# Layer 3's preparation spread over its steps, and a bank of TensorE filled between two halves of a sum

## The chip, the cores and the metric

The kernel runs on one core of one Trainium2 chip. The metric is device time in microseconds (us), the median of several runs. One further execution was recorded by the hardware profiler; all profile lines come from it.

## The reference

A small network of four layers runs on a batch of four images, each 256 channels of 64 x 64 points. Every layer normalizes its input in groups of channels, computes something, and adds it to its input. Layers 0 to 2 (a deformable convolution, an attention, a second deformable aggregation) are not touched. Layer 3 is a selective state space model over the 4096 points of an image in sequence, here cut to what matters:

```python
xz = einsum('bld,ed->ble', xs, in_proj_w)             # 256 -> 2 * 512
u, res = split(xz, 2)
u = silu(causal_depthwise_conv(u, conv_w) + conv_b)   # 4 taps
dt, Bm, Cm = split(einsum('bld,ed->ble', u, x_proj_w), [16, 32])
delta = softplus(einsum('blr,dr->bld', dt, dt_proj_w) + dt_proj_b)
# for each of 512 channels d and 16 states n, along the sequence l:
state = exp(delta * A[d, n]) * state + delta * Bm[n] * u
y = sum_n(state * Cm[n]) + u * D
out = einsum('ble,de->bld', y * silu(res), out_proj_w)
```

## The kernel before

The images are worked one after the other, and within an image the layers. `layer3` cuts the sequence into NC = 8 chunks of C = 512 points. The 512 channels lie as four quarters `dc` of 128 partitions. A chunk is worked in 16 steps, one for each state n, so an image has 128 steps `s`. In one step:

- TensorE (PE) spreads row n of B over the partitions: `bn`, one matmul in bf16 (`state`, L1460). `bn` has a single PSUM bank.
- VectorE (DVE) multiplies `h = du * bn` (the product, L1537), for all four quarters (128x2048) or for three (128x1536). In the second case GpSimd (POOL) multiplies the fourth (`quarter`, L1468) with a row `bs` that a DMA has spread. The list `helped` says in which steps: 14, 15 and 0 to 5 of each chunk.
- ScalarE (ACT) computes `da = exp(delta * A)` for each quarter (L1547), into one of two PSUM banks, and DVE scans over the points (L1548), four scans a step.
- POOL copies the last column to `carry` (L1560) and multiplies `h` by the spread row of C, `cn` (L1563).
- PE adds `h` into four PSUM banks `y` with an identity matrix as weights (`add`, L1438), two steps later. In state 0 it also adds `u * D` (L1436).

`front(j)` prepares chunk j while chunk j-1 is worked: the normalized input `xn`; four projections into `up`, through the one PSUM bank of the pool `ps` (`project`, matmuls L1242, copies L1246); four convolutions, each as four matmuls with diagonal weights (`convolve`, L1285, copied by ACT at L1290); SiLU of `u` and of the gates of the chunk before, with a load of ACT's tables before and after (`silu`, L1299, L1258; called the table visit below); the product that gives dt, B and C (`shares`, L1309, copied to `dbc`); `step` (L1324, ACT at L1330 and L1331), and then a softplus in whole-tile steps, of which ACT does the functions and POOL three additions (L1346, L1355, L1356) and `du = delta * u` (L1357). `gate` projects the other half of `xz`, and `split` cuts B into bf16 parts. `close(j)` multiplies the finished `y` by the gates and projects them to the output, after `gated` (L1514, four products on DVE).

Each part is put by hand into a slot: a step and a half of it. `front(j)` starts LEAD = 4 steps before chunk j; for chunk 1, prepared in part by `first`, 2 steps are taken off. The main loop fixes the order on every engine, as the pools are under a manual schedule; in short:

```python
product; empty(s, -1); gated
scan(0); scan(1); quarter(s + 1)
empty(s, 0)          # second PE parts of the slot, and ACT's copy of the bank
fill(s, 1)           # PE's part of the second half
scan(2); scan(3)
empty(s, 1)
carry; h * cn; empty(s, 2)
state(s + 1); add(s - 2); fill(s + 1, 0)
```

All engines take their queues in order. `first()` prepares chunk 0 by itself before the steps begin: quarters 1 and 3 are convolved by DVE (L1159, L1161), 0 and 2 by PE (L1177); POOL casts the weights `pick` (L1110) and normalizes `xn` of chunk 1 (L1169); then, quarter by quarter, softplus passes from ACT (L1220 to L1222, L1215) to DVE (L1223, L1224, L1216, L1217) and POOL (L1227, L1209 to L1212).

Of the kernel before, what the change touches and what calls it, by code (L numbers as in the profile page):

```python
# [16 lines left out]
P = 128  # L17
# [46 lines left out]
class Net:  # L64
# [1016 lines left out]
    def layer3(self, x, out, nxt, early):  # L1081
# [5 lines left out]

        nc, tc = self.nc, self.tc
        C = 512
        NC, LEAD = N // C, 4  # L1090
        with (
# [18 lines left out]
            nc.gpsimd.tensor_copy(pick.rearrange("p n m -> p (n m)"), rows.rearrange("p a b -> p (a b)"))  # L1110
# [9 lines left out]
            kept = pa.tile([P, 2, C], F32, tag="kept", name="kept")  # L1120
# [9 lines left out]
            def first():  # L1130
# [23 lines left out]
                for dc in range(4):  # L1154
                    pu = spare()
                    project(pu, xn, dc)
                    if dc % 2:
                        nc.vector.tensor_copy(up[:, dc, 3:], pu)
                        nc.vector.tensor_scalar_mul(u[:, dc, :], up[:, dc, :C], cw[:, dc, 0:1])  # L1159
                        for i in range(1, 4):  # L1160
                            nc.vector.scalar_tensor_tensor(  # L1161
                                u[:, dc, :], up[:, dc, i : i + C], cw[:, dc, i : i + 1], u[:, dc, :], ALU.mult, ALU.add
                            )
                    else:
                        nc.scalar.copy(up[:, dc, 3:], pu)
                for ct in range(2):
                    if ct == 0:
                        c1["xn"] = pa.tile([P, 2, C], F32, tag="xn3", name="xn3")
                    nc.gpsimd.tensor_scalar(  # L1169
                        c1["xn"][:, ct, :], x[:, ct, C : 2 * C], rs[:, ct : ct + 1], shift[:, ct : ct + 1], ALU.mult, ALU.add  # L1170
                    )
                nc.gpsimd.tensor_copy(tail, up[:, :, C : C + 3])
                px = bank()
                for dc in (0, 2):
                    cv = spare()
                    for i in range(4):
                        nc.tensor.matmul(cv, conv[:, dc, i, :], up[:, dc, i : i + C], start=(i == 0), stop=(i == 3))  # L1177
                    nc.scalar.activation(u[:, dc + 1, :], u[:, dc + 1, :], AF.Silu, bias=cb[:, dc + 1 : dc + 2])
                    nc.scalar.activation(u[:, dc, :], cv, AF.Silu, bias=cb[:, dc : dc + 1])
                for k, dc in enumerate((1, 3, 0, 2)):  # L1180
                    nc.tensor.matmul(px, xpw[:, dc, :], u[:, dc, :], start=(k == 0), stop=(k == 3))
# [17 lines left out]

                c["gates"] = [spare() for _ in range(4)]  # L1200
                for dc, pg in enumerate(c["gates"]):
                    project(pg, xn, 4 + dc)
# [5 lines left out]
                def split(lo, hi):  # L1208
                    nc.gpsimd.tensor_copy(bp[lo:hi], dbc[lo:hi])  # L1209
                    if hi < P:  # L1210
                        nc.gpsimd.tensor_copy(t[hi:], dbc[hi:])
                        nc.gpsimd.tensor_sub(dbc[hi:], dbc[hi:], t[hi:])  # L1212

                def end(dc):
                    nc.scalar.activation(w[:, dc, :], w[:, dc, :], AF.Ln)  # L1215
                    nc.vector.tensor_add(delta[:, dc, :], delta[:, dc, :], w[:, dc, :])  # L1216
                    nc.vector.tensor_mul(du[:, dc, :], delta[:, dc, :], u[:, dc, :])  # L1217

                for dc in range(4):
                    nc.scalar.activation(w[:, dc, :], pzs[dc], AF.Abs, bias=dtb[:, dc : dc + 1])  # L1220
                    nc.scalar.activation(du[:, dc, :], w[:, dc, :], AF.Exp, scale=-1.0)
                    nc.scalar.activation(delta[:, dc, :], pzs[dc], AF.Relu, bias=dtb[:, dc : dc + 1])  # L1222
# [4 lines left out]
                    nc.gpsimd.tensor_sub(delta[:, dc, :], delta[:, dc, :], du[:, dc, :])  # L1227
                    if dc < 3:
                        split(*((0, 64), (64, 96), (96, 128))[dc])
                    if dc:  # L1230
                        end(dc - 1)
                end(3)
                for dc in range(3):
                    nc.scalar.copy(c1["up"][:, dc, 3:], pus[dc])

# [24 lines left out]
            def front(j):  # L1260
# [17 lines left out]
                for dc in range(4):  # L1278
                    put((dc + 1) // 2, (dc + 1) % 2, *project(j, dc, lambda dc=dc: c["up"][:, dc, 3:]))

                def convolve(dc):
# [7 lines left out]
                    def rest():  # L1289
                        nc.scalar.activation(c["u"][:, dc, :], c["b"], AF.Identity, bias=cb[:, dc : dc + 1])  # L1290
                        if dc == 0:
# [4 lines left out]
                for dc in range(4):  # L1296
                    put(2 + dc, 1, *convolve(dc))
# [5 lines left out]
                put(6, 0, None, silu)  # L1303
# [14 lines left out]
                put(7, 1, shares, keep)  # L1318
# [16 lines left out]
                for dc in range(4):  # L1335
                    put(8 + dc // 2, dc % 2, *step(dc))
                put(10, 0, None, lambda: nc.scalar.activation(c["du"], c["du"], AF.Exp, scale=-1.0))

                def one():
                    c["w"] = pa.tile([P, 4, C], F32, tag="w3", name="w3")  # L1340
                    nc.scalar.activation(c["w"], c["du"], AF.Identity, bias=self.ones[:, 0:1])

                put(10, 1, None, one)


                put(10, 2, None, lambda: nc.gpsimd.tensor_add(c["delta"], c["delta"], c["du"]))  # L1346
                put(
                    12,
                    0,
                    None,  # L1350
                    lambda: nc.scalar.activation(c["du"], c["w"], AF.Identity, bias=self.ones[:, 0:1], scale=-1.0),
                )
                put(13, 0, None, lambda: nc.scalar.activation(c["w"], c["w"], AF.Ln))
                last = 17 if j > 1 else 15
                put(13, 2, None, lambda: nc.gpsimd.tensor_add(c["delta"], c["delta"], c["du"]))  # L1355
                put((13 + last) // 2, 2, None, lambda: nc.gpsimd.tensor_add(c["delta"], c["delta"], c["w"]))  # L1356
                put(last, 2, None, lambda: nc.gpsimd.tensor_mul(c["du"], c["delta"], c["u"]))  # L1357

                for dc in range(4):
                    at = ((14, 0), (14, 1), (15, 0), (15, 1)) if j > 1 else ((10, 1), (11, 0), (11, 1), (12, 1))  # L1360
                    put(*at[dc], *gate(j, dc))
# [19 lines left out]
                for i in range(3):  # L1381
                    put((11, 12, 14)[i], i % 2, None, split(i))
                return todo

            def close(j):
# [5 lines left out]
                def project(ot):  # L1391
                    def pe():
# [6 lines left out]
                        xs = kept[:, ot, :] if last else x[:, ot, bass.ts(j, C)]  # L1399
                        nc.tensor.matmul(c["b"], self.ident, xs, start=False, stop=True)  # L1400

                    def rest():
                        to = kept if last else x[:, :, bass.ts(j, C)]
# [5 lines left out]
                for ot in range(2):  # L1409
                    todo.append((11 + 2 * ot - LEAD, 1, *project(ot)))  # L1410
                if not last:
                    todo.append((15 - LEAD, -1, None, lambda: fetch(j)))

                    todo.append((13 - LEAD + DS if j < NC - 2 else 17 - LEAD, -1, None, lambda: count(j)))
# [12 lines left out]
            def keep():  # L1427
                for ct in range(2):
                    nc.scalar.copy(kept[:, ct, :], x[:, ct, bass.ts(NC - 1, C)])

            def add(j, n, h):
                c = chunks[j]
                if n == 0:
                    c["ys"] = [py.tile([P, C], F32, tag="y", name="y") for _ in range(4)]
                    for dc in range(4):
                        nc.tensor.matmul(c["ys"][dc], diag[:, dc, :], c["u"][:, dc, :], start=True, stop=False)  # L1436
                for dc in range(4):
                    nc.tensor.matmul(c["ys"][dc], self.ident, h[:, dc, :], start=False, stop=(n == DS - 1))  # L1438


            hs, helped = {}, (14, 15, 0, 1, 2, 3, 4, 5)
# [261 lines left out]
```

## Time and profile before

| | |
|---|---|
| time, median of 3 runs | 9832.72 us (9831.53 to 9837.35) |
| the profiled execution: its time | 9825.3 us |
| its span, first to last instruction | 9823.5 us |
| busy: PE, DVE, ACT, POOL | 8552.6, 7522.1, 4893.9, 7112.0 us |
| mean granted clock of TensorE | 0.959 |
| first product of layer 3, image 1 and image 4 | at 1563.67 and 8864.99 us |
| last instruction of DVE's scans, image 4 | starts at 9792.2 us |

A line of a timeline gives start and length in us, engine, line of the kernel, operation, output and inputs, and how many instructions are merged; in brackets stands the idle time of the engine just before, and what ended it. A line of a group of instructions ends with busy time, mean duration in ns, and idle time before. A line of the windows gives, for a stretch of time, each engine's busy time.

### The profile page before, as it was taken

The page shows a single profiled execution, that of the slowest core. Times are in us where ns is not written, and L with a number is a line of the kernel's source. Part 1 is how long each engine was busy: PE and PEld are TensorE (multiplying, and loading weights), DVE is VectorE, ACT ScalarE, POOL GpSimd, SP SyncE. Part 2 cuts the span into 40 slices and gives each one's busy share as a digit, 9 for nine tenths or more (in the row PEclk, how much of TensorE's full clock was granted, in tenths as well). Part 3 has the DMA queues.
Part 4 walks back from the last instruction along what each step waited for, and adds up shares of the span by engine and source line. Part 5 has one row for each costly group of instructions (what it writes and reads, how often), then busy time and mean ns, then how long its engine had stood idle before and what let it go on. Part 6 is the DMA issues. An engine that isn't in the chain of part 4 may idle for free. (4 is left out here: it accounts for less than half of the span.)

```text
span 9823.5 us, 89566 instructions
## 1 busy us (share of the span) xinstructions
PE 8552.6 (87%) x29129; PEld 4208.7 (43%) x29129; DVE 7522.1 (77%) x8175; ACT 4893.9 (50%) x7532; POOL 7112.0 (72%) x4220
## 2 busy tenths in 40 slices
PE   5789998998778999899878899989987889998997
PEld 3643343333464344333346434433334643443333
DVE  4764498999676459899968645989996764689998
ACT  3753335665474333566547433266655733326664
POOL 3746687888474668798857467789985746778997
PEclk9999999999899999999989999999998999999999
DMA  7840011222783001122279201122228820111221
GB/s 255 319 158 1 26 50 56 64 62 67 257 320 139 1 30 47 58 63 63 67 272 333 107 1 35 51 57 62 62 64 313 324 73 1 39 51 55 60 60 51
DMA packets 415274, 1024.78 MB, mean 104 GB/s; under 512 B 38771, under 2 KB 111916, under 8 KB 412748
## 3 DMA queue, kind: packets, MB, share of 16 engines
q0 software_dynamic: 165888, 604.05, 17.0%
q1 hardware_dynamic: 248908, 414.90, 13.7%
q8 instruction: 233, 3.82, 0.2%
q14 instruction: 245, 2.01, 0.1%
HBM read 851.70 MB, written 93.37 MB: 96 GB/s over the span
## 5 line engine op out<-in xcount | busy, mean ns | idle before, releaser
L1548 DVE TENSOR_TENSOR_SCAN h<-da,carry,h 128x512 f32<-128x512 f32 x2048 | 2469.0, 1264 | 138.3 <-ACT da L1547 78.0
L1563 POOL TENSOR_TENSOR h<-h,cn 128x2048 f32<-128x2048 f32 x508 | 2299.7, 4527 | 41.3 <-POOL carry L1560 0.8
L1547 ACT ACTIVATE da<-delta,l3a 128x512 f32<-128x512 f32 x2048 | 1393.1, 689 | 1064.1 <-DVE h L1548 1061.5
L1438 PE MATMUL y<-h,ident 128*128 128x512 f32 x4096 | 1907.6, 610 | 12.4 <-POOL h L1563 12.4
L344 POOL DMA_INDIRECT g<-tab,idx x1152 | 1359.8, 1180 | 748.6 <-issue 367.5
L565 POOL TENSOR_TENSOR acc<-acc,e 128x1024 f32<-128x1024 f32 x480 | 1126.0, 2346 | 539.5 <-ACT e L561 517.6
L388 PE MATMUL pz<-cols,l0w 128*128 128x256 f32 x4608 | 1211.3, 409 | 184.6 <-DVE cols L377 73.9
L1438 PEld LDWEIGHTS y<-h,ident 128*128 128x128 f32 x4096 | 801.7, 196 | 1251.6 <-issue 1166.7
L353 DVE SCALAR_TENSOR_TENSOR r<-g,wx,r 128x512 f32<-128x512 f32 x1152 | 858.4, 745 | 373.4 <-ACT r L352 251.4
L462 DVE TENSOR_REDUCE m<-pm 128x3 f32<-128x1536 f32 (+2 forms) x340 | 599.5, 1763 | 699.9 <-PE pm L452 699.9
L1537 DVE TENSOR_TENSOR h<-du,bn 128x2048 f32<-128x2048 f32 (+1 forms) x512 | 1022.8, 1998 | 49.9 <-PE bn L1460 49.8
L388 PEld LDWEIGHTS pz<-cols,l0w 128*128 128x128 f32 x4608 | 893.2, 204 | 353.7 <-DVE cols L377 110.4
L561 ACT ACTIVATE e<-sc 128x1024 f32<-128x1024 f32 x512 | 496.1, 1020 | 1029.5 <-PE sc L548 1029.5
L572 PE MATMUL cx<-e,v 128*128 128x512 f32 x2048 | 1001.0, 616 | 0.0
L845 DVE TENSOR_TENSOR prod<-ring,A 128x1280 f32<-128x1280 f32 x640 | 922.4, 1480 | 77.9 <-DMA ring<-ring 60.2
L352 ACT ACTIVATE r<-g,wx 128x512 f32<-128x512 f32 x1152 | 826.5, 717 | 265.0 <-DMA g<-tab,idx 211.6
L862 PE MATMUL pacc<-prod,ident 128*128 128x512 f32 x1920 | 914.5, 611 | 32.8 <-DVE prod L845 21.8
L854 POOL TENSOR_TENSOR prod<-prod 128x512 f32<-128x512 f32 x640 | 801.2, 1277 | 182.2 <-DVE prod L845 157.3
L370 PE MATMUL pt<-ident,acc 128*128 128x128 f32 x2304 | 428.3, 293 | 295.0 <-DVE acc L361 234.2
L572 PEld LDWEIGHTS cx<-e,v 128*128 128x128 f32 x2048 | 352.4, 189 | 599.3 <-issue 596.8
L360 ACT ACTIVATE acc<-r,wy 128x256 f32<-128x256 f32 x1152 | 571.3, 496 | 16.5 <-DVE r L353 13.7
L361 DVE SCALAR_TENSOR_TENSOR acc<-r,wy,acc 128x256 f32<-128x256 f32 x1152 | 548.6, 477 | 0.0
(255 smaller groups left out, 10767.4 us busy)
## 6 DMA issues: line engine op xcount, KB each, us to landing
cn<-cd SPq DMA_DIRECT2D x512, 256.0 KB
tab<-vt SPq DMA_DIRECT2D x112, 640.0 KB
bs<-cd SPq DMA_DIRECT2D x256, 256.0 KB
ring<-ring SPq DMA_DIRECT2D x288, 126.0 KB
ring<-ring SPq DMA_DIRECT2D x288, 124.0 KB
g<-tab,idx POOLq DMA_INDIRECT x1152
x<-in_x SPq DMA_DIRECT2D x64, 256.0 KB
out<-x SPq DMA_DIRECT2D x56, 256.0 KB
```

The lines of the kernel that those rows point to most:

```text
L344: nc.gpsimd.indirect_dma_start(out=g[:], out_offset=None, in_=tab[:, :], in_offset=bass.IndirectOffsetOnAxis(ap=idx[:, t, k : k + 1], axis=0),
L353: nc.vector.scalar_tensor_tensor(r, g[:, :, 1, :], wx[:, 1, t, k : k + 1], r, ALU.mult, ALU.add)
L388: nc.tensor.matmul(sums[m][:, ot, :256], wf[:, i, bass.ts(ot, P)], cols[m][:, i, :], start=(i == 0), stop=(i == 17),)
L565: nc.gpsimd.tensor_add(b["acc"], b["acc"], e)
L572: nc.tensor.matmul(blocks[qb]["cx"], v[:, 4 * (i + kt // 4 * 4) + kt % 4, :], e[:, bass.ts(i % 2, 512)], start=(kt == 0 and i == 0), stop= ...
L845: nc.vector.tensor_mul(d["prod"][:, :, t, :].rearrange("p x (g c) -> p x g c", c=GC), ring[y // VR % 4][:, :, y % VR, :].rearrange("p x (g ...
L862: nc.tensor.matmul(d["pd"], self.ident, prod[:, wx, :], start=(wy == 0 and wx == 4), stop=(wy == WIN - 1 and wx == 2),)
L1438: nc.tensor.matmul(c["ys"][dc], self.ident, h[:, dc, :], start=False, stop=(n == DS - 1))
L1537: nc.vector.tensor_mul(h[:, :d, :], c["du"][:, :d, :], c.pop(("bn", n)).to_broadcast([P, d, C]))
L1547: nc.scalar.activation(da, c["delta"][:, dc, :], AF.Exp, scale=al[:, dc, n : n + 1])
L1548: nc.vector.tensor_tensor_scan(h[:, dc, :], da, h[:, dc, :], carry[:, dc, n : n + 1], ALU.mult, ALU.add)
L1563: nc.gpsimd.tensor_mul(h, h, cn.to_broadcast([P, 4, C]))
```

## The change

All of it is in `layer3`.

- The slots move. LEAD is 5. Projections of `up` stand at steps (counted from the first) 0, 1, 1 and 4 instead of 0 to 2; convolutions at 2, 3, 5 and 6 instead of 2 to 5; SiLU, `shares`, `step` and most of the softplus one step later than in the old count, thus at the same step of the chunk before; for chunk 1 one step later. Some parts of ACT move by half a step. Gates and `close` come one step earlier.
- In the main loop `state(s + 1)` moves from the end of the step to between the scans. `add` is cut into two halves of two quarters, and `fill(s + 1, 0)` goes between them. Where the slot's first half holds nothing for PE, `fill(s, 1)` goes ahead of `state`.
- At the steps of the table visit (`visits`) DVE makes the next step's product between scans 1 and 2. bn_stats of the next image's input (`count`) moves there too for most chunks.
- `quarter` writes a tile of its own, `hq`; steps 14 and 15 of chunk 0 are no longer helped.
- In `first`, DVE convolves quarters 1, 3 and 0, PE only 2. `pick`, `xn` of chunk 1 and the casts of `split` go from POOL to ACT. Relu and Ln write PSUM in place, and DVE makes the subtraction of POOL. The gates' projections follow `state(0)`.
- `kept` uses the buffer of `xn3`.

```diff
-        NC, LEAD = N // C, 4
+        NC, LEAD = N // C, 5
...
-                for dc in range(4):
+                c1["xn"] = pa.tile([P, 2, C], F32, tag="xn3", name="xn3")
+                for dc in (1, 3, 0, 2):
                     pu = spare()
                     project(pu, xn, dc)
-                    if dc % 2:
+                    if dc == 1:
                         nc.vector.tensor_copy(up[:, dc, 3:], pu)
+                    else:
+                        nc.scalar.copy(up[:, dc, 3:], pu)
+                    if dc != 2:
                         nc.vector.tensor_scalar_mul(u[:, dc, :], up[:, dc, :C], cw[:, dc, 0:1])
...
+                    if dc == 3:
+                        nc.scalar.copy(pick.rearrange("p n m -> p (n m)"), rows.rearrange("p a b -> p (a b)"))
...
+                px, cv = bank(), spare()
+                for i in range(4):
+                    nc.tensor.matmul(cv, conv[:, 2, i, :], up[:, 2, i : i + C], start=(i == 0), stop=(i == 3))
+                for k, dc in enumerate((1, 2, 3, 0)):
+                    nc.scalar.activation(u[:, dc, :], cv if dc == 2 else u[:, dc, :], AF.Silu, bias=cb[:, dc : dc + 1])
                     nc.tensor.matmul(px, xpw[:, dc, :], u[:, dc, :], start=(k == 0), stop=(k == 3))
...
                 def end(dc):
-                    nc.scalar.activation(w[:, dc, :], w[:, dc, :], AF.Ln)
-                    nc.vector.tensor_add(delta[:, dc, :], delta[:, dc, :], w[:, dc, :])
+                    nc.scalar.activation(pzs[dc], w[:, dc, :], AF.Ln)
+                    nc.vector.tensor_add(delta[:, dc, :], pzs[dc], delta[:, dc, :])
                     nc.vector.tensor_mul(du[:, dc, :], delta[:, dc, :], u[:, dc, :])
...
-                    nc.gpsimd.tensor_sub(delta[:, dc, :], delta[:, dc, :], du[:, dc, :])
-                    if dc < 3:
-                        split(*((0, 64), (64, 96), (96, 128))[dc])
+                    nc.vector.tensor_sub(delta[:, dc, :], pzs[dc], du[:, dc, :])
                     if dc:
                         end(dc - 1)
+                        split(*((0, 64), (64, 96), (96, 128))[dc - 1])
...
                 for dc in range(4):
-                    put((dc + 1) // 2, (dc + 1) % 2, *project(j, dc, lambda dc=dc: c["up"][:, dc, 3:]))
+                    at = ((0, 1), (1, 0), (1, 1), (4, 1))[dc]
+                    put(*at, *project(j, dc, lambda dc=dc: c["up"][:, dc, 3:]))
...
                 for dc in range(4):
-                    put(2 + dc, 1, *convolve(dc))
+                    at = ((2, 1) if j > 1 else (3, 0), (3, 1), (5, 1), (6, 1))[dc]
+                    put(*at, *convolve(dc))
...
-                put(6, 0, None, silu)
+                put(7, 0, None, silu)
+                visits.append(DS * (j - 1) + (2 if j > 1 else 5))
...
-                last = 17 if j > 1 else 15
-                put(13, 2, None, lambda: nc.gpsimd.tensor_add(c["delta"], c["delta"], c["du"]))
-                put((13 + last) // 2, 2, None, lambda: nc.gpsimd.tensor_add(c["delta"], c["delta"], c["w"]))
-                put(last, 2, None, lambda: nc.gpsimd.tensor_mul(c["du"], c["delta"], c["u"]))
+                last = 18 if j > 1 else 16
+                put(14, 2, None, lambda: nc.gpsimd.tensor_add(c["delta"], c["delta"], c["du"]))
+                put((14 + last) // 2, 2, None, lambda: nc.gpsimd.tensor_add(c["delta"], c["delta"], c["w"]))
+                put(last, 2, None, lambda: nc.gpsimd.tensor_mul(c["du"], c["delta"], c["u"]))
...
-            hs, helped = {}, (14, 15, 0, 1, 2, 3, 4, 5)
+            hs, helped = {}, [s for s in range(NC * DS) if s % DS in (14, 15, 0, 1, 2, 3, 4, 5) and s // 2 != 7]
...
                     scan(0)
                     scan(1)
                     quarter(s + 1)
+
+                    free = not any(pe or rest.__name__ == "begin" for pe, rest in slots.get((s, 0), ()))
+                    if free:
+                        fill(s, 1)
+                    state(s + 1)
+                    if s in visits:
+                        product(s + 1)
                     empty(s, 0)
-                    fill(s, 1)
+                    if not free:
+                        fill(s, 1)
                     scan(2)
                     scan(3)
                     empty(s, 1)
...
-                    state(s + 1)
                     late.append((j, n, h))
-                    if len(late) > 2:
-                        add(*late.pop(0))
+
+                    a = late.pop(0) if len(late) > 2 else None
+                    if a:
+                        add(*a, 0)
                     fill(s + 1, 0)
+                    if a:
+                        add(*a, 1)
```

`product(s)` is the old product, moved into a function that does nothing where it has already been called.

## Prediction before the run

> **What bounds the kernel now.** Only layer 3 changes; it runs once per image, four times. First I read the windows by stage of the last image's layer 3, cut at the first product of each chunk.
>
> ```profile
> core 0: us, PE busy (x) PEld busy (x) DVE busy (x) ACT busy (x) POOL busy (x), PEclk, DMA share, GB/s
> 8818.00:8865.00 47.00, 37.93 (x85) 16.47 (x85) 29.98 (x41) 21.00 (x33) 29.92 (x39) 0.93 0.23 77
> 8865.00:8984.60 119.60, 100.22 (x230) 41.92 (x231) 108.12 (x81) 75.90 (x106) 97.50 (x47) 0.99 0.17 47
> ...
> 9215.80:9332.40 116.60, 107.00 (x253) 45.78 (x253) 110.51 (x85) 74.35 (x103) 105.61 (x49) 1.00 0.20 60
> ```
>
> A middle chunk takes 116.6 us; DVE is busy 110.5 of it, PE 107.0, POOL 105.6. DVE paces it, with little room behind. Its gaps are in the timeline of DVE at the end of one chunk and the start of the next:
>
> ```profile
> 9201.25 1.73 DVE L1537 TENSOR_TENSOR h<-du,bn 128x1536 f32<-128x1536 f32 x1
> 9203.08 4.81 DVE L1548 TENSOR_TENSOR_SCAN h<-da,carry,h 128x512 f32<-128x512 f32 x4
> 9208.74 1.75 DVE L1537 TENSOR_TENSOR h<-du,bn 128x1536 f32<-128x1536 f32 x1 [0.85 <-PE bn L1460]
> ...
> 9215.82 1.75 DVE L1537 TENSOR_TENSOR h<-du,bn 128x1536 f32<-128x1536 f32 x1 [0.42 <-PE bn L1460]
> ...
> 9238.71 2.46 DVE L1548 TENSOR_TENSOR_SCAN h<-da,carry,h 128x512 f32<-128x512 f32 x2 [2.21 <-ACT da L1547]
> 9241.08 1.73 DVE L1537 TENSOR_TENSOR h<-du,bn 128x1536 f32<-128x1536 f32 x1
> ...
> 9247.64 1.73 DVE L1537 TENSOR_TENSOR h<-du,bn 128x1536 f32<-128x1536 f32 x1
> ```
>
> A free step with a 3-wide product lasts 6.56 (9241.08 to 9247.64), with a 4-wide one 7.09. The stalled steps last 7.49 and 7.08. So DVE's own need is 8 x 6.55 + 8 x 7.09 + 2.39 (four gate products) = 111.5 a chunk, and 5 us are waits. PE's timeline shows why:
>
> ```profile
> 9208.54 3.60 PE L1438 MATMUL y<-h,ident 128*128 128x512 f32 x8
> 9211.97 3.60 PE L1285 MATMUL front<-up,conv 128*128 128x512 f32 x8
> 9215.41 0.38 PE L1460 MATMUL bn<-bp,pickn 128*128 128x512 bf16 x1
> ```
>
> A convolution (3.43 from start to start), the sum over states (3.43) and bn (0.21) make 7.07, more than DVE's 6.55, in four steps running; step 14 also holds a projection. Last, the timeline of ACT at the start:
>
> ```profile
> 8844.40 0.59 ACT L1184 COPY dbc<-front 128x512 f32<-128x512 f32 x1 [1.45 <-PE front L1181]
> ...
> 8861.50 0.63 ACT L1215 ACTIVATE w<-w 128x512 f32<-128x512 f32 x1 [4.38 <-DVE du L1224]
> ```
>
> and that of POOL there and late in the first chunk:
>
> ```profile
> 8858.57 1.59 POOL L1227 TENSOR_TENSOR delta<-delta,du 128x512 f32<-128x512 f32 x1
> ...
> 8977.66 4.51 POOL L1357 TENSOR_TENSOR du<-delta,u 128x2048 f32<-128x2048 f32 x1
> ```
>
> ACT idles 4.38 while each quarter of delta goes round through DVE, POOL and ACT; the first product starts at 8864.99. The du that opens the second chunk is ready at 8982.2, and its product starts at 8984.63. All times below are of the last image.
>
> **Waits of the later chunks.** The waits on bn: five chunk ends, each 0.94 + 3 x 0.53 = 2.5 us, 12.6. The new order puts convolutions at 13.5, 14.5, 0.5, 1.5 and the fourth projection at 15.5. PE's needs are then 7.07 in steps 12 to 14, 5.36 in 15, 7.07 in 0 to 3, 5.36 in 4 and 5, 7.93 in 6 and 8, 3.64 in 7. bn(s+1) may run once product(s) has ended, 4.7 us before DVE wants it; step 7 with its 3.64 sets that lead back to full. Added up from there, and counted from the end of each step's product, the next bn is ready at 0.8 in step 8, 0.4 in 12, 2.1 in 13, 2.6 in 14, 1.4 in 15, 2.0 and 2.5 in 0 and 1, 2.6 in 6: always 2 us before DVE asks. The bank's copies on ACT fall between the two halves of the sum (1.72), so PE waits little for the bank. Gone: 12.6.
>
> The waits at the table visit: 1.38 in chunk 1 and 5 x 2.21, 12.4. ACT's chain (load, two SiLUs, load) takes 6.3; DVE has two scans and four gate products beside it. The early product adds 1.83 to DVE there and leaves the next step without one: 2.21 - 1.83 = 0.4 would remain, but ACT now comes to the visit some 0.5 earlier, as PE no longer holds up the last copy. Taken as gone. Behind the early product wait the scans, and it needs bn(s+1), which now stands right behind the sum: PE reaches it 4 us early. bn_stats (2 x 0.69) moves there too in images 1 to 3: the same DVE work. Six small waits of 0.18 on ACT also go, 1.1.
>
> What may take their place: ACT's step 6 holds two copies of the last delta row, two casts and the exponential, 4.4 us against 4.4 of room; POOL delivers the quarter for step 15 26.0 us after scan 3 of step 11 (9187.07 to 9213.02), and DVE will want it after 26.2. From 0 to 1.5 us a chunk; I take 0.3, the sums being about even, 1.8 for six. Balance: 12.6 + 12.4 + 1.1 - 1.8 = **24.3**.
>
> **Start.** One convolution is left to PE, three go to DVE: 2.86 each (mul and three adds, 8836.97 to 8839.83). They begin when POOL has cleared up (8831.1) and end at 8839.7; SiLU ends at 8840.5, the table load at 8841.8, dbc is copied from there instead of 8844.40: 2.6 gained. POOL's pick cast (1.90) and xn (2.11) go to ACT, where projections and the one convolution (3.43) cover them; uncovered they would cost some 3.5. Then the chain per quarter: DVE takes 0.43 + 4 x 0.69, without the 1.0 to 1.6 of both when POOL worked beside it, and POOL's 1.59 leaves the chain; ACT takes 1.82 + 0.52 + casts of 1.2. Four quarters: from 8843.3 to 8858.5. Product 0 moves from 8865.0 to 8858.6: **6.4** gained (4 to 8: POOL's two subtractions still slow DVE at 1.0 to 1.5). The gate projections now stand behind bn(0).
>
> delta now reads PSUM twice a quarter: the gate products from PSUM take 0.680 (L1514), additions from SBUF 0.68 where POOL rests (L1216 at 8863.67), so the sum takes no difference. [...]
>
> **First chunk.** Gains: the visit's wait of 4.41 falls to about 2.4 (a 4-wide product, 2.36, is moved in; a late convolution gives some back). Steps 14 and 15 keep the fourth quarter on DVE: 2 x 0.53 = 1.06 lost. But POOL's three additions to delta and the product du stand a step later: carry 12, three h of 4.76 with their carries and three of 4.49 make 27.8 us after scan 3 of step 12, while DVE has only three steps, 21.3, until it wants du for product 16. So DVE waits 6.5 us there, where before it waited 0.99 + 2.61 + 0.49. PE may also be late early on, since it idles some 4.5 us before bn(0): in the last chunk eight matmuls took 5.29 instead of 3.60 after 3.28 us idle (9663.77), but 3.59 after 2.42, so 0 to 1.7; I take half. [...] Sum: 109.1 of DVE work, 1.06, 0.85, 2.4, 6.5 and some 0.9 of small waits as before (0.39 + 0.49) make 120.8 instead of 119.6, **1.2 lost** (from 3.5 lost to 1 won).
>
> **Sum.** 24.3 + 6.4 - 1.2 = 29.5 an image, 118 in four: 9825.3 of the profiled execution becomes 9707. The timed median lies 7.4 above that execution, so 9832.7 - 118 = **9715**. The last chunk and the tail keep their work. Of the moved DMAs, x is fetched a step earlier behind its store, as before; eight bs loads vanish; nobody waits.
>
> **Rivals.**
> 1. *POOL becomes the bound.* Its busy 105.6 us a chunk against 111.5 leaves 5; if the quarter or h come late by 1 to 2 us in each of six chunks, or du later than reckoned, 36 us go: about 9751. Against it: POOL idles 4 us at the visit and catches up.
> 2. *The early product does not fill the visit*, because bn(s+1) or the h buffer is late: 6 x 1.83 x 4 = 44 remain, 9759. Against: the buffer's reader ends a step before.
> 3. *Slower: ACT blocks DVE.* A copy of the bank that waits for PE holds up the exponentials queued behind it on ACT, as at the first visit (4.41). The new order puts a projection or convolution in the second half behind bn in six steps of sixteen (steps 4, 5, 9 to 12). It decides once each is 0.7 us late beyond ACT's 3.2 us of room (29.5 over seven chunks of six); at 1.2 late, 50 us an image stand against 29.5 won: 9915. For that such a front must end over 5 us after the product; I get 2.1 to 2.4.
> 4. *No effect*: PE at 104.6 us of work is near DVE's 111.5; a granted clock of 0.90 would make it the bound at 116 and leave only start and first chunk, 4 x 5.2: 9812. The rows show 0.99 to 1.00.
>
> **Chances.** Forecast 0.76 (own range 9696 to 9742, from the bounds above, not all at their ends at once), rival 1 0.10, rival 2 0.05, rival 3 0.05, rival 4 0.04. The range takes the forecast's and rival 1's: 9696 to 9752. About 0.2% (20 us) is what a measurement can tell from no change: faster 0.91, same 0.04, slower 0.05.
>
> **Right or wrong by.** In the profile after: chunk starts 111.5 to 112 apart; under DVE's scans no wait on ACT at the visits, under the product none on bn at chunk ends, but one on POOL of some 6 us at product 16; product 0 some 34 us after xn instead of 40. Periods over 114, or waits of scans on ACT in steps 4 to 12, would make it wrong.

## The result, and the profile after

| | before | after |
|---|---|---|
| time, median of 4 runs each | 9835.03 us (9831.53 to 9849.14) | 9721.13 us (9708.01 to 9733.23) |
| ratio | | 0.9881 (95% interval 0.9864 to 0.9898) |
| the profiled execution | 9825.3 us | 9708.0 us |
| idle time before the scans, four images | 138.3 us | 83.7 us |
| idle time before the products, four images | 49.9 us | 26.7 us |

The kernel is faster by 1.2%. The idle times of the table come from the profiles, which list the instructions in groups. Before and after the change the groups of the scans and of the products read (busy time, mean ns, idle time before them and what ended most of it):

```profile
L1548 DVE TENSOR_TENSOR_SCAN h<-da,carry,h 128x512 f32<-128x512 f32 x2048 | 2469.0, 1264 | 138.3 <-ACT da L1547 78.0
L1537 DVE TENSOR_TENSOR h<-du,bn 128x2048 f32<-128x2048 f32 (+1 forms) x512 | 1022.8, 1998 | 49.9 <-PE bn L1460 49.8
```

```profile
L1562 DVE TENSOR_TENSOR_SCAN h<-da,carry,h 128x512 f32<-128x512 f32 x1800 | 2172.5, 1264 | 83.7 <-ACT da L1560 35.3
L1480 DVE TENSOR_TENSOR h<-du,bn 128x2048 f32<-128x2048 f32 (+1 forms) x512 | 1025.0, 2002 | 26.7 <-POOL du L1382 24.8
```

After the change 248 of the 2048 scans, those that read `hq`, stand in a group of their own, with no idle time before them. Under the product (L1480 now) the releaser was PE's bn in 49.8 us of 49.9. It is now POOL's du in 24.8, that is 6.2 an image at one place. Under the scans (L1562) the share put down to ACT fell from 78.0 to 35.3 us.

The windows of the last image's layer 3 after the change, cut at the normalized input, at the first product of chunks 0, 1 and 2, and for a middle chunk:

```profile
core 0: us, PE busy (x) PEld busy (x) DVE busy (x) ACT busy (x) POOL busy (x), PEclk, DMA share, GB/s
8734.90:8769.30 34.40, 27.83 (x57) 11.60 (x58) 23.13 (x36) 25.12 (x38) 9.21 (x17) 0.90 0.17 48
8769.30:8895.30 126.00, 111.79 (x257) 47.50 (x256) 109.20 (x82) 77.00 (x109) 98.60 (x44) 0.97 0.15 45
8895.30:9006.40 111.10, 102.90 (x244) 44.47 (x244) 109.64 (x84) 73.24 (x101) 102.04 (x48) 1.00 0.19 58
9117.60:9228.80 111.20, 106.32 (x253) 45.99 (x252) 109.74 (x86) 73.93 (x102) 105.47 (x49) 1.00 0.20 62
```

A middle chunk now lasts 111.2 us with DVE busy for 109.7 of it: DVE does hardly anything but its own work. The first chunk went the other way, 126.0 where it was 119.6. Two timelines show both. First DVE's around the start of a middle chunk, where each product waited 0.42 to 0.85 for bn and the third scan of the third step 2.21 for ACT:

```profile
9111.05 1.73 DVE L1480 TENSOR_TENSOR h<-du,bn 128x1536 f32<-128x1536 f32 x1
...
9117.61 1.73 DVE L1480 TENSOR_TENSOR h<-du,bn 128x1536 f32<-128x1536 f32 x1
...
9124.17 1.73 DVE L1480 TENSOR_TENSOR h<-du,bn 128x1536 f32<-128x1536 f32 x1
...
9134.76 2.45 DVE L1562 TENSOR_TENSOR_SCAN h<-da,carry,h 128x512 f32<-128x512 f32 x2
9137.13 1.72 DVE L1480 TENSOR_TENSOR h<-du,bn 128x1536 f32<-128x1536 f32 x1
9138.78 1.27 DVE L1562 TENSOR_TENSOR_SCAN h<-da,carry,h 128x512 f32<-128x512 f32 x1
```

The products stand 6.56 apart, with no bracket. In the visit (9134.76 on) the next step's product lies between the second and the third scan, and the third scan follows it without a wait. PE does the same work there as before, but ahead of time:

```profile
9121.43 3.60 PE L1443 MATMUL y<-h,ident 128*128 128x512 f32 x8
9124.86 3.60 PE L1285 MATMUL front<-up,conv 128*128 128x512 f32 x8
9128.30 0.38 PE L1465 MATMUL bn<-bp,pickn 128*128 128x512 bf16 x1
9128.51 3.60 PE L1443 MATMUL y<-h,ident 128*128 128x512 f32 x8
9132.50 0.38 PE L1465 MATMUL bn<-bp,pickn 128*128 128x512 bf16 x1 [0.39 <-DVE h L1480]
```

A step of 7.07 is still longer than DVE's 6.56, but the stretch begins with a lead, and at its end (9132.50) PE waits for DVE and not DVE for PE. Then DVE's timeline late in the first chunk:

```profile
8854.29 2.46 DVE L1562 TENSOR_TENSOR_SCAN h<-da,carry,h 128x512 f32<-128x512 f32 x2 [1.75 <-ACT da L1560]
...
8862.36 2.46 DVE L1562 TENSOR_TENSOR_SCAN h<-da,carry,h 128x512 f32<-128x512 f32 x2 [3.43 <-ACT da L1560]
...
8870.42 4.81 DVE L1562 TENSOR_TENSOR_SCAN h<-da,carry,h 128x512 f32<-128x512 f32 x4 [0.81 <-ACT da L1560]
...
8895.26 1.75 DVE L1480 TENSOR_TENSOR h<-du,bn 128x1536 f32<-128x1536 f32 x1 [5.85 <-POOL du L1382]
```

The last line was forecast (6.5). The three waits on ACT in steps 11 to 13, 6.1 us with a small one of 0.15 left out here, were not. ACT's timeline and PE's say what ACT did there:

```profile
8852.16 1.52 ACT L1270 ACTIVATE xn<-x,shift,rs 128x512 f32<-128x512 f32 x2 [2.88 <-PE front L1241]
8853.59 1.28 ACT L1560 ACTIVATE da<-delta,l3a 128x512 f32<-128x512 f32 x2
8854.82 0.57 ACT L1245 COPY sres<-front 128x512 f32<-128x512 f32 x1
8859.26 0.59 ACT L1245 COPY up<-front 128x512 f32<-128x512 f32 x1 [3.87 <-PE front L1241]
```

```profile
8850.25 1.88 PE L1241 MATMUL front<-xn,l3a 128*128 128x512 f32 x4
8855.44 3.78 PE L1241 MATMUL front<-xn,l3a 128*128 128x512 f32 x4 [3.31 <-ACT sres L1245]
```

Chunk 2's `begin` (8852.16) writes the one `xn3` buffer. It waits 2.88 for the last gate product of chunk 1 (PE, 8850.25), which still reads it: that gate's slot is 11.5, the `begin`'s is 11.0. The exponentials of the third and fourth quarter stand behind it in ACT's queue. Then chunk 2's first projection, in the same slot 11.5, waits 3.31 for the gate's copy. PE comes back slow: the projection takes 3.78 where the gate product took 1.88, and the granted clock is 0.50 from 8855.4 to 8859.2 and 1.00 from 8850.2 to 8852.1. The copy of that projection (8859.26) holds up ACT again, 3.87.

### The profile page after: what moved, and what is told of

Same layout as the page of the kernel before. It is cut to its first block, busy times and chain, and to the rows that moved or that the text cites. A ratio compares the mean times of both kernels' runs of the same rounds, so it can differ in the third digit from the quotient of the medians.

```text
span 9706.1 us, 89200 instructions
## 1 busy us (share of the span) xinstructions
PE 8526.4 (88%) x29097; PEld 4207.1 (43%) x29097; DVE 7498.5 (77%) x8203; ACT 4909.6 (51%) x7568; POOL 7032.0 (72%) x4164
## 5 line engine op out<-in xcount | busy, mean ns | idle before, releaser
L1562 DVE TENSOR_TENSOR_SCAN h<-da,carry,h 128x512 f32<-128x512 f32 x1800 | 2172.5, 1264 | 83.7 <-ACT da L1560 35.3
L1443 PE MATMUL y<-h,ident 128*128 128x512 f32 x4096 | 1931.5, 607 | 11.7 <-POOL h L1585 11.7
L1480 DVE TENSOR_TENSOR h<-du,bn 128x2048 f32<-128x2048 f32 (+1 forms) x512 | 1025.0, 2002 | 26.7 <-POOL du L1382 24.8
## 6 DMA issues: line engine op xcount, KB each, us to landing
ring<-ring SPq DMA_DIRECT2D x288, 126.0 KB
```

The source lines that it names most:

```text
L1443: nc.tensor.matmul(c["ys", dc], self.ident, h[:, dc, :], start=False, stop=(n == DS - 1))
L1480: nc.vector.tensor_mul(h[:, :d, :], c["du"][:, :d, :], c.pop(("bn", n)).to_broadcast([P, d, C]))
L1562: nc.vector.tensor_tensor_scan(h[:, dc, :], da, hb, carry[:, dc, n : n + 1], ALU.mult, ALU.add)
```

## The experiments

The 15 executions of the kernel before on one chip lie between 9832.00 and 9864.55 us. The two profiled executions of the change are 12.1 apart (9708.0 and 9720.1), though the start and chunks 0 to 6 of their last image agree to 0.15. Four of the runs (no early product, bn late, old slots, before + preparation) were made on a chip where the other layers take less time (the kernel before: 9661.67 there). Layer 3 has the same durations on both (chunks 1 to 6: 696.97 us in before + preparation there, 697.03 in the kernel before here). So small effects are read in the stages of the last image's layer 3, and the whole time as a ratio to the kernel before on the same chip.

The last image is not like the other three. In images 1 to 3 DVE also makes the bn_stats of the next image in chunks 2 to 6, and a middle chunk of the change lasts 112.35 there, not 111.2. What an edit is worth can differ with it. So where the text gives a sum over four images, it adds up the differences of chunks 0 to 6 in each of the four; it does not multiply the last image by four.

| kernel | xn to product 0 | chunk 0 | chunks 1 to 6 | chunk 7 to end | ratio (95%) |
|---|---|---|---|---|---|
| before | 40.16 | 119.64 | 697.03 | 141.84 | 1 |
| after | 34.36 | 125.99 | 668.08 | 142.76 | 0.9881 (0.9864 to 0.9898) |
| after, again | 34.36 | 125.99 | 668.23 | 141.48 | 0.9874 (0.9859 to 0.9890) |
| no early product | 35.92 | 128.19 | 677.53 | 142.61 | 0.9911 (0.9887 to 0.9935) |
| bn late | 35.78 | 124.14 | 668.27 | 141.26 | 0.9875 (0.9851 to 0.9899) |
| sum whole | 34.58 | 127.86 | 670.51 | 141.32 | 0.9903 (0.9887 to 0.9920) |
| old slots | 34.54 | 122.48 | 678.81 | 141.23 | 0.9901 (0.9877 to 0.9924) |
| old slots, sum whole | 35.94 | 123.20 | 684.92 | 141.41 | 0.9912 (0.9897 to 0.9927) |
| before + preparation | 36.00 | 127.02 | 696.97 | 141.60 | 1.0008 (0.9998 to 1.0018) |
| before + preparation and copies | 35.83 | 125.70 | 698.37 | 141.64 | 1.0004 (0.9995 to 1.0013) |
| gates half a step earlier | 35.57 | 122.02 | 668.08 | 141.31 | 0.9880 (0.9864 to 0.9897) |
| du a step earlier | 34.48 | 120.14 | 668.06 | 141.29 | 0.9861 (0.9842 to 0.9880) |
| both | 34.68 | 116.28 | 668.67 | 141.38 | 0.9859 (0.9843 to 0.9876) |
| du, and the last gate alone | 34.37 | 114.91 | 668.88 | 142.85 | 0.9842 (0.9829 to 0.9856) |

**The early product taken out.**

```diff
-                    if s in visits:
-                        product(s + 1)
```

> The change with the early product taken out; its bn still stands right behind the sum. Theory (the early product fills DVE's time while ACT is at the table visit): the wait under the third scan comes back at each of the later six visits, some 1.7 us (2.21 before, less the 0.5 by which ACT now comes earlier), and the first visit's wait of 2.23 grows by the 2.26 of the product to about 4.5: 12.5 us an image, 50 in four, 9771 against 9721 for the change. Rival (the visits' waits went because ACT comes earlier, and the early product is not needed): within 10 of 9721.

Measured: 0.9911 against 0.9881, about 29 us in place of 50. In the last image's stages it is 9.5 us over chunks 1 to 6 and 2.2 in chunk 0, 11.7 together. DVE's timeline at a middle visit there:

```profile
8879.04 2.45 DVE L1562 TENSOR_TENSOR_SCAN h<-da,carry,h 128x512 f32<-128x512 f32 x2
8882.87 1.28 DVE L1562 TENSOR_TENSOR_SCAN h<-da,carry,h 128x512 f32<-128x512 f32 x1 [1.38 <-ACT da L1560]
```

The wait comes back, with 1.38 in each of six visits (1.7 expected) and 4.41 in the first. So the early product fills it, and rival 2 falls. The other 0.8 of the 2.21 stays away without it; that ACT arrives earlier fits this, but was not tried alone.

In images 1 to 3, from chunk 2 on, most of the wait does not come back, as bn_stats stands in the same gap. This is the same visit in image 2 of the same run:

```profile
4134.50 2.45 DVE L1562 TENSOR_TENSOR_SCAN h<-da,carry,h 128x512 f32<-128x512 f32 x2
4136.86 1.27 DVE L152 BATCH_NORM_STATS2 st<-x 128x6 f32<-128x512 f32 x2
4138.33 1.28 DVE L1562 TENSOR_TENSOR_SCAN h<-da,carry,h 128x512 f32<-128x512 f32 x1 [0.20 <-ACT da L1560]
```

The early product is worth only 5.8 to 6.3 us there. The four images make 29.5, as the ratio has it. The expectation of 50 had taken the last image for all four.

**bn issued late again.**

```diff
-                    state(s + 1)
                     if s in visits:
+                        state(s + 1)
                         product(s + 1)
...
                     empty(s, 2)
+                    if s not in visits:
+                        state(s + 1)
                     late.append((j, n, h))
```

> The change with bn(s+1) issued at the end of step s again, except at the visits; on PE this puts bn behind the second-half front in the steps that have a first-half part (4, 5, 9 to 12) and nowhere else. Theory (the chunk ends were cured by where the convolutions lie, and in steps 4, 5 and 9 to 12 bn has 4.7 us of lead): within 8 of 9721. Rival (the early bn is what took the 12.6 us of bn waits away): about 9771.

Measured: 0.9875, and 668.27 against 668.08 in chunks 1 to 6. Behind a second-half front or not, bn is in time there; with the new slots, its place in the queue is not what cures the chunk ends. In the first chunk the run is 1.9 shorter than the change: the large waits on ACT in steps 11 and 12 are gone or small there, and one of 1.85 on bn stands in their place.

**Old slots**, **the sum whole**, and **both**.

```diff
-                    at = ((0, 1), (1, 0), (1, 1), (4, 1))[dc]
+                    at = ((1, 1), (2, 0), (2, 1), (3, 0))[dc] if j > 1 else ((0, 1), (1, 0), (1, 1), (4, 1))[dc]
...
-                    at = ((2, 1) if j > 1 else (3, 0), (3, 1), (5, 1), (6, 1))[dc]
+                    at = ((3, 1), (4, 1), (5, 1), (6, 1))[dc] if j > 1 else ((3, 0), (3, 1), (5, 1), (6, 1))[dc]
```

```diff
                     if a:
                         add(*a, 0)
-                    fill(s + 1, 0)
-                    if a:
                         add(*a, 1)
+                    fill(s + 1, 0)
```

> The change with the projections and convolutions of chunks 2 to 7 in the kernel before's slots (projections 12.5, 13, 13.5, 14; convolutions 14.5, 15.5, 0.5, 1.5); the early xn, the halves and the early bn stay. It also keeps the first projection of chunk 2 away from chunk 1's last gate product. Theory (the slots cured the chunk ends): waits of the product on bn come back at the starts of chunks 2 to 6, up to 2.5 us each, 10 to 12.6 an image, 40 to 50 in four; the first chunk gives back up to 3.3 an image of its ACT waits: 9750 to 9771. Rival (the halves, which let a bank's copy pass during the sum, cured them): 9705 to 9725.

> The change with the sum over states issued whole again, ahead of the next step's first-half front. Only steps with a first-half part are touched (4, 5, 9, 10, 12). Theory (the halves give the bank's copy time to pass, and PE has room in these steps anyway): 0 to 2 us an image, ratio to the kernel before 0.988 to 0.989. Rival (sum 3.43, two projections of 1.72 and bn 0.21 make 7.08 of PE against a DVE step of 7.09, so a copy that PE waits for makes bn late by 0.5 in each of two or three steps a chunk): 1 to 1.5 us a chunk, some 10 an image, ratio 0.992.

> Old slots for the projections and convolutions of chunks 2 to 7 and the sum whole again; the early bn, the early products and the preparation stay. Old slots alone made a middle chunk 113.3 to 113.7 us (111.2 to 111.5 in the change), the whole sum alone 111.6 to 111.9. Theory (the two are separate shares of the 2.5 us of bn waits): about 113.7 to 114.1. Rival (each covers for the other, so that the waits of before come back only with both gone): 114.5 to 116.5.

With the old slots the waits on bn are back at the chunk start, by DVE's timeline of chunk 2:

```profile
8854.47 1.75 DVE L1480 TENSOR_TENSOR h<-du,bn 128x1536 f32<-128x1536 f32 x1 [0.30 <-PE bn L1465]
...
8861.55 1.75 DVE L1480 TENSOR_TENSOR h<-du,bn 128x1536 f32<-128x1536 f32 x1 [0.42 <-PE bn L1465]
...
8868.64 1.75 DVE L1480 TENSOR_TENSOR h<-du,bn 128x1536 f32<-128x1536 f32 x1 [0.42 <-PE bn L1465]
...
8877.36 1.28 DVE L1562 TENSOR_TENSOR_SCAN h<-da,carry,h 128x512 f32<-128x512 f32 x1 [0.56 <-ACT da L1560]
```

Middle chunks are 113.3 to 113.7 long, 2.1 above the change; 10.7 an image. The first chunk returns 3.5 of it, as expected: chunk 2's first projection no longer shares a slot with the last gate, and of the waits in steps 11 to 13 only the first is left. That is 7.2 in the last image. Images 1 to 3 lose 3.6 to 4.3 each, since the wait of 0.56 on ACT does not appear there, and the four make 19; by the ratio it is about 20. The expectation, 29 to 50, had the right cause and too much of it.

The whole sum alone costs 0.4 a chunk, 2.4 an image, and 1.9 in the first chunk (a second wait on ACT in step 12), 4.3 together. In images 1 to 3 it is 1.7 to 2.5. The four make 10, nearer to the theory (0 to 2 an image) than to the rival (some 10 an image). The ratio gives some 22, but its interval overlaps with that of the change.

With both, a middle chunk takes 114.5, 3.3 above the change and 0.7 more than the two together: partly each covers for the other. The value lies at the lower edge of the rival's range, so neither reading holds alone. Over chunks 1 to 6 of all four images it is the same: the old slots cost 32.7, the whole sum 4.7 and both 49.3. The slots are the larger share by far. The wait of 0.85 that step 15 had before the change stays away even with both; bn's earlier place may be what does that, but old slots with bn late were not run.

**The preparation alone**: the kernel before with the whole `first()` of the change, which holds `state(0)` and the cast of `pick` itself.

```diff
-            nc.gpsimd.tensor_copy(pick.rearrange("p n m -> p (n m)"), rows.rearrange("p a b -> p (a b)"))
...
                 first()
                 for s in range(2):
                     ahead(s)
-                state(0)
                 quarter(0)
```

> The kernel before with the change's preparation alone (three convolutions on DVE, xn and casts on ACT, the subtraction from PSUM, the gate projections behind bn(0)). Theory (the start is worth what the trace shows, 40.2 to 34.4 us from xn to the first product, and nothing gives it back): 5.8 an image, 23 in four, 9835 - 23 = 9812; ratio 0.9976. Rival (the cold PE and the later gate products give it back in the first chunk): 9825 to 9835.

Measured: 1.0008. Product 0 does come after 36.0 instead of 40.2, but the first chunk takes 7.4 more: a wait of 6.01 under the third scan of step 0 and a longer one in step 9 (2.06 in place of 0.58). So the theory fell. The rival, which let the later gate products give the gain back in the first chunk, had the place right.

**The preparation and the copies of the gates.**

```diff
-                slots.setdefault((i, 0), []).append((None, gates))
+                slots.setdefault((i, 1 - i), []).append((None, gates))
```

> The kernel before with the change's preparation and, of its other edits, only the copies of chunk 0's gates out of PSUM half a step and a whole step later (second half of step 0, first half of step 1). Theory (the preparation alone lost its 5.8 us to a 6.01 us wait in step 0, because ACT's copies of gates 0 and 1 wait there for gate products that now stand behind bn(0), with the exponentials of the third and fourth quarter queued behind them): the 6.01 us wait shrinks to under 1, first chunk back from 127.0 to 119.6 to 121, ratio 0.9976 to 0.9985. Rival (the wait is that of the front's projection on PE, whose nine us of gate products come first, and stays): ratio 1.000.

The theory fell again: 1.0004, 4.94 of the 6.01 stay, and the first chunk takes 125.7. ACT's timeline and PE's in this run show the rival's wait:

```profile
8865.82 1.33 ACT L1545 ACTIVATE da<-delta,l3a 128x512 f32<-128x512 f32 x2
8874.33 0.59 ACT L1245 COPY up<-front 128x512 f32<-128x512 f32 x1 [7.18 <-PE front L1241]
8874.81 1.31 ACT L1545 ACTIVATE da<-delta,l3a 128x512 f32<-128x512 f32 x2
```

```profile
8863.16 0.59 PE L1459 MATMUL bn<-bp,pickn 128*128 128x512 bf16 x1 [4.55 <-ACT bp L1203]
8863.54 9.04 PE L1151 MATMUL front<-xn,l3a 128*128 128x512 f32 x16
8872.41 1.88 PE L1241 MATMUL front<-xn,l3a 128*128 128x512 f32 x4
```

ACT copies the fourth projection of chunk 1 in step 0 (slot 0.0 in the old list), and PE does that projection behind 9.04 us of gate products, which now follow bn(0). The exponentials of the third and fourth quarter stand behind the copy. In the change that projection stands at step 2.5, and no such wait is in its trace. That the shorter preparation is worth something only together with chunk 1's new slots follows from this, but is not shown by itself: no run gave the kernel before the preparation and that one slot.

**The two mends of the first chunk.** Chunk 1's gate products half a step earlier; POOL's three operations for chunk 1 a step earlier; both; and POOL's with the last gate alone moved.

```diff
-                    at = ((14, 0), (14, 1), (15, 0), (15, 1)) if j > 1 else ((11, 1), (12, 0), (12, 1), (13, 1))
+                    at = ((14, 0), (14, 1), (15, 0), (15, 1)) if j > 1 else ((11, 0), (11, 1), (12, 0), (12, 1))
```

```diff
-                last = 18 if j > 1 else 16
-                put(14, 2, None, lambda: nc.gpsimd.tensor_add(c["delta"], c["delta"], c["du"]))
+                last = 18 if j > 1 else 15
+                put(14 if j > 1 else 13, 2, None, lambda: nc.gpsimd.tensor_add(c["delta"], c["delta"], c["du"]))
```

```diff
-                    at = ((14, 0), (14, 1), (15, 0), (15, 1)) if j > 1 else ((11, 1), (12, 0), (12, 1), (13, 1))
+                    at = ((14, 0), (14, 1), (15, 0), (15, 1)) if j > 1 else ((11, 1), (12, 0), (12, 1), (13, 0))
```

> The change with chunk 1's four gate products in the first chunk half a step earlier (steps 9, 9.5, 10, 10.5 instead of 9.5, 10, 10.5, 11.5), so that none lies behind the begin of chunk 2 (its xn takes the same buffer) or shares a slot with its first projection. Theory (the begin waits on ACT for the last gate product, the projection on PE for that gate's copy, and the exponentials stand behind both): the waits of scans on ACT in steps 11 and 12 (1.75, 3.43, 0.15) go; product 16 stays 27.8 us behind scan 3 of step 12, so 5.3 us an image, 21 in four, ratio 0.9881 - 0.0022 = 0.9859. Rival (ACT is simply full in these steps, with the exponential over four rows, Ln and casts): 0 to 2 an image, ratio 0.987 to 0.988.

> The change with chunk 1's two additions to delta and its du on POOL one step earlier (11, 12 and 13 instead of 12, 13 and 14). Theory (27.8 us of POOL's queue behind scan 3 of step 12 set product 16): the additions then start behind h of step 11, du is ready some 3 us before DVE asks, the 5.85 us wait at product 16 goes, the ACT waits of steps 11 to 13 stay: 5.85 an image, 23 in four, ratio 0.9857. Rival (POOL waits for ACT's Ln or for u, and is no earlier): ratio 0.988.

> Both edits: gate products half a step and POOL's three operations a step earlier. Theory (two separate waits in a row): from product 0 to product 16 about 115 us instead of 126, 11 us an image, 45 in four, ratio 0.9881 - 0.0046 = 0.9835, below both kernels. By counting POOL from scan 3 of step 11 (six operations with carries, 27.8) du is ready 0.6 us before DVE wants it, so up to 1.5 us of it may stay. Rival (POOL then holds up h of steps 14 to 16 instead): some 6 us an image, ratio 0.9857.

> POOL's three operations for chunk 1 a step earlier, as in the run with both edits, and of chunk 1's gate products only the last moved, half a step (11.0 instead of 11.5): it stands at the end of step 10, ahead of the begin. Theory (the last gate product behind the begin is the whole cause of the ACT waits in steps 11 to 13): those waits stay away, and the wait of 1.17 in step 9 that came with moving all four goes: first chunk 115 us, 1.2 below both edits; ratio 0.983 to 0.986. Rival (the gate's copy in front of the begin's xn makes ACT late in step 11): a wait of 1 to 3 us there, first chunk 117 to 119.

> The change itself once more, so that it stands on the same chip and in the same rounds as the version with both edits mended. Ratio 0.988; first chunk 126 us, product 0 some 34.4 to 35.8 us after xn. If the versions differ as their traces do, the other is 10 to 11 us an image faster, 40 to 45 in all.

With the gates earlier no scan waits for ACT in steps 11 to 13; one of 1.16 appears in step 9, where ACT also has an exponential over four rows (1.91) and two casts. Chunk 0 falls by 4.0 (5.3 expected). The whole time (0.9880) does not show it, and its interval holds 16 us less as well as none; in the profiled execution the last image's layer 3 began 18 us later than in the change's, though layer 3 of the three images ahead took 14 us less there. With du earlier the 5.85 wait is gone and chunk 0 falls by 5.85, as expected. Both together: 116.3, 9.7 less (11 expected). Its ratio, 0.9859, lies at the rival's value and not at the 0.9835 of the theory, but the stages of the four images come to 36.5 us, and the wait at product 16 shrinks to 0.86. The run with du alone keeps the waits on ACT, 6.2 us of them:

```profile
8857.79 2.46 DVE L1562 TENSOR_TENSOR_SCAN h<-da,carry,h 128x512 f32<-128x512 f32 x2 [1.75 <-ACT da L1560]
...
8865.86 2.46 DVE L1562 TENSOR_TENSOR_SCAN h<-da,carry,h 128x512 f32<-128x512 f32 x2 [3.43 <-ACT da L1560]
```

With the last gate also moved, to slot 11.0, no scan waits on ACT in steps 9 to 13. The gate's product then stands ahead of the `begin`, as the change sorts the parts of a slot so that those with work for PE come first. ACT's timeline there, and DVE's at product 16:

```profile
8835.41 0.59 ACT L1245 COPY sres<-front 128x512 f32<-128x512 f32 x1
8835.90 1.52 ACT L1270 ACTIVATE xn<-x,shift,rs 128x512 f32<-128x512 f32 x2
8837.51 0.69 ACT L1560 ACTIVATE da<-delta,l3a 128x512 f32<-128x512 f32 x1
```

```profile
8870.27 1.75 DVE L1480 TENSOR_TENSOR h<-du,bn 128x1536 f32<-128x1536 f32 x1 [0.91 <-POOL du L1382]
```

The `begin` (8835.90) waits for nothing, and what is left at product 16 is 0.91 on POOL, with 0.47 more for POOL's quarter before that step's fourth scan. Chunk 0 takes 114.9, 11.1 below the change and 5.2 below du alone. Side by side on the same chip this version took 9686.11 us (9682.01 to 9699.66) and the change 9720.13 (9712.98 to 9730.00): 34 us less, with no overlap (40 to 45 expected; the stages of the four images give 41). It beats both kernels, by 1.6% against the one before. It differs from the change in the slot of one gate product and in the step of three operations on POOL.

## Why the prediction was right

The forecast was 9715 and 9707 for the profiled execution; measured were 9721 and 9708.0. Its 29.5 us an image stand against 27.5 in the last image's layer 3 (5.8 - 6.35 + 28.95 - 0.9). Without the last chunk, the four images add up to 111 of the 117 that the profiled executions differ by; the rest lies outside. Two terms were off and nearly cancelled, so that the total came out this close was in part luck. The 0.9 is the end of the last image; a second profile of the change does not show it (141.48).

- **Start**, 6.4 forecast: 5.8 here, and 4.4 to 6.8 over the four images. dbc is copied 2.4 earlier after xn (2.6 forecast), and the rest is the shorter chain per quarter. It was costed as if it stood by itself; the preparation-only runs show that the gain can be lost behind it.
- **First chunk**, 1.2 lost forecast, 6.35 measured. This is the mis-sized term. Its parts that were named came out: the visit 2.23 (2.4 forecast), du 5.85 (6.5), the cold PE 0.66 (0.85). What failed is "some 0.9 of small waits as before": there were 6.1 on ACT. The mechanism was the prediction's own rival 3, a copy that waits for PE with exponentials behind it, and its own sign of error ("waits of scans on ACT in steps 4 to 12"), but in one chunk of eight. It was judged for the slots of chunks 2 to 7, where the last reader of `xn3` stands at 10.5; chunk 1's own list, with the last gate at 11.5 against a `begin` at 11.0, was not followed through. Between the run with du alone and the one with that gate moved as well, all 6.2 us of these waits go: this was the whole cause.
- **Later chunks**, 24.3 forecast, 28.95 measured. The bn waits, 12.6, were right. The visits gave 14.4 instead of 12.4: steps 2 and 3 of a middle chunk took 11.10 + 6.56 before and 6.40 + 8.72 after, 2.54 less, where the bracket alone said 2.21. A step lasted longer than without a wait by more than the bracket, and for bn the prediction had used step lengths, for the visits the brackets. The small waits of step 8 come to 0.29 each in the same way, not 0.18. The 1.8 held back for new waits did not appear, but for one of 0.46 in each of chunks 4 to 6 (last section). Chunk 4 had lost another 1.3 in the kernel before, which the sum did not count. In images 1 to 3, with bn_stats, middle chunks went from 117.5 to 117.8 down to 112.35, and chunks 1 to 6 gained 28 to 29.
- **Rival 1** (POOL bound): POOL is busy 105.5 of 111.2 and no wait on it shows in chunks 1 to 6; it binds in chunk 0 alone, as forecast. **Rival 2** (the early product does not fill the visit): the run without it refutes it. **Rival 4** (no effect): the granted clock is 1.00 in each of chunks 1 to 5 and 0.97 in chunk 6, which lasts 111.3.
- **PSUM as a source**: DVE's addition with one source in PSUM takes 0.68 (L1211). Its product from SBUF right behind it takes 0.69 where POOL rests (L1212 at 8767.34). Beside an operation of POOL the same product took 1.42 and 1.22 (8759.72 and 8763.63). The sum took no difference for PSUM, and these rows show none.
- **The cold PE**: after 4.55 us idle, bn and the 16 gate matmuls took 8.53 to the next bn, where 7.07 would do (0.21 and four projections of 1.72). That is 1.46 late, at a granted clock of 0.83; 0.66 of it reached DVE, as a wait on ACT in step 1. Over the four images of the change's profile and the last image of five more (bn late, gates half a step earlier, both, du and the last gate alone, the change again), the stretch takes 8.53 to 9.27 and the wait is 0.65 to 1.40. The wait is the stretch less 7.85 to 7.88 each time, so DVE had some 0.8 of room and paid the rest. The prediction's range was 0 to 1.7, and it took half, 0.85: the waits lie within it. Its two rows don't make the length of the idle time the cause: in the kernel before, the sum over states took 3.59 after 2.42 idle (9628.25), but also 5.29 after 2.42 (9393.95) and 3.59 after 2.75 (9677.10).

## What to carry to other kernels

When parts are moved between slots, walk every list that shares a buffer or a bank, the special first chunk's above all: one reader half a step behind the writer of a single buffer cost about as much as the whole preparation won. A gain at the start is worth what the queue behind it lets through, so a part of a change measured alone can be worth nothing. Before the stages of one image stand for all, see what the others do there: bn_stats in the same gap took half the worth of the early product. Cost a removed wait by the length of the step with it and without it, not by the bracket.

## What had not been expected

The first projections of `first` took 8.52 us in one execution and 9.94 in another with the same code there, and the granted clock differs with it. These are the windows of those projections and of the softplus behind them, after the change and with bn late:

```profile
8735.50:8744.10 8.60, 8.52 (x16) 3.51 (x16) 3.96 (x7) 2.89 (x4) 5.61 (x12) 0.83 0.00 0
8744.10:8766.00 21.90, 16.14 (x36) 6.60 (x37) 15.36 (x23) 19.61 (x30) 3.01 (x4) 0.99 0.26 76
```

```profile
8558.00:8568.10 10.10, 9.94 (x16) 4.05 (x16) 5.41 (x10) 2.92 (x4) 5.63 (x12) 0.72 0.00 0
8568.10:8590.00 21.90, 16.14 (x36) 6.61 (x37) 13.99 (x22) 19.62 (x30) 3.14 (x4) 0.95 0.25 76
```

The clock is 0.83 in the one and 0.72 in the other, the stretch behind takes 21.9 in both, and product 0 comes 34.36 or 35.78 after xn: the 1.42 goes through whole. In the runs with this preparation the start lies between 34.4 and 36.0, also from image to image of one execution (35.85, 35.83, 34.50 and 34.36 in the change's profile), so a start read once is known only to some 1.6 us. What sets how long PE stays slow after its idle time (2.84 and 2.83 before these projections) stays open. Open, too, is a gap of 0.46 before a scan that the last image shows every 18 steps from chunk 4 on (at 9287.02, 9412.71, 9538.41 and 9663.57), at the same steps in all versions of the change but the one without early products. Other images, and the kernel before, show such gaps at other steps.
